# Evictions of the projections ahead of all other work on ScalarE and VectorE, in a fused three-layer graph attention kernel

## The chip, the cores and the metric

The kernel runs on one core of one Trainium2 chip, all in float32. The metric is the device time in microseconds (us). TensorE multiplies matrices into PSUM[...]; ScalarE and VectorE read results out of PSUM and do the element-wise work; GpSimd does element-wise work in SBUF; SyncE issues most DMAs.

## The reference

64 graphs of 256 nodes with 512 features each, and a 256x256 adjacency matrix per graph. Three attention layers follow each other; the second and the third belong to one reference layer.

```
Q, K, V = (x @ W + b) by 8 heads of 64
scores = Q K^T / 8 + a_i + c_j + b_g + log(adj + 1e-9)
x = softmax(scores) V + x

# twice: W1 with 8 heads, then W2 with one head of 512
h = layer_norm(x, g, b) @ W
s = h . a_src ; t = h . a_dst
e = leaky_relu(s_i + t_j, 0.2) + adj
x = softmax(e) h + x
```

## The kernel before

All 64 graphs go through one software pipeline on one core. `graph(b)` is a Python generator that traces the work of one graph and stops at each `yield`. A list, `order`, says which graph takes its next step; in the steady part it repeats the table `period`, whose entries are pairs (age, step): the steps of graphs of ages 0 to 5 are interleaved, so in each period every stage of some graph runs once. `start` and `finish` are lists of their own for the first and the last graphs.

TensorE executes exactly in the order in which its instructions are traced (`manual_schedule` for that engine). For ScalarE, VectorE, GpSimd and the DMA queue a planner makes the lists before the run: it walks a model of the program in time, and when an engine is free, it gives it, of the instructions whose inputs are there in that model, the one with the best priority. Without further marks priority is the order of tracing: what was traced earlier goes first. On the chip each engine then runs its fixed list in order and waits on semaphores.

Each projection (V, Q, K of the first layer, V1 of the second, V2 of the third) is one call of `winograd` (L310): a 2x2 block product done with seven products instead of eight, accumulated in three PSUM banks a, b and c. `product` (L322) issues the matmuls of one of the seven, on line L326 where the result lies by token (V, V1, V2) and L333 where it lies by column (Q, K). Between the products the banks are read out, and these readings are the evictions the change speaks of:

- `kept` (L339) copies a bank's intermediate sum into an SBUF tile (m1, m5, u2), since the bank goes on accumulating. Its instruction is on ScalarE: L525 for V and K, L558 for Q (two pieces), L639 for V1 and V2.
- `put` writes a finished block into V, QT, KT, V1 or V2. When a kept tile is to be added it is on VectorE (L537, L567, L575, L648); the last block of each projection, with nothing to add, goes over ScalarE (L535, L558, L573, L646).

The order in `winograd` is: products 1 into a, 5 into b, 2 into c, 6 into a, 3 into b (entry "K" in the table, for example), then 7 into a (entry "K7"), then 4 into a (entry "K4"). Product 6 adds to bank a and so must wait until m1 has been copied from it; product 7 likewise waits for u2, product 4 for the put of a.

Other work on the same two engines, by its lines:

- Scores of the first layer ("scores", "mask"): 16 matmuls for each half of the heads (L592), eight exponentials on ScalarE (L599), then on VectorE four multiplications by the adjacency (L613) and two sums over the halves, `total` (L618). `weight_sums` ("sums 0") sums `total` on TensorE into ps_su (L384); "product 0" multiplies by V into ps_num (L425); "gather 0" scales it on VectorE (L434, L438).
- Weights of the second layer ("weights", eight entries per period): for each head two ReLU of R on ScalarE (L676); after every second head VectorE adds the adjacency (L682) and ScalarE takes four exponentials (L686); after every fourth head VectorE sums the halves into R (L691), which ps_su reads in "sums 1". R comes by a DMA (L473) that the DMA queue issues when its buffer is free.
- Third layer: L744, the products with V2 into ps_av (L756), reciprocals (L761), scaling on ScalarE (L764), addition on GpSimd (L765).
- Statistics for the norms on VectorE (L258 to L290), among them "tokens" and "gather" entries; transposes of X and the adjacency (L501, "turn").

The order of the entries is the table's: in program order "Q4" and "K" come after the fourth "weights" and before the fifth, and "V2" comes between the two "mask" entries.

Of the kernel before, what the change touches and what calls it, by code (L numbers as in the profile page):

```python
# [20 lines left out]
def kernel(  # L21
# [130 lines left out]
    with ExitStack() as main:  # L152
# [6 lines left out]
        def ps(tag):  # L159

            return psum.tile([P, 512], F32, name=f"ps_{tag}", tag="ring", bufs=8)
# [148 lines left out]
        def winograd(left, w, by_token, keep, put, banks="cba"):  # L310

            width = HD if not by_token else w.shape[-1]
            bank = {n: ps(n)[:, :width] for n in banks}
            a, b, c = bank["a"], bank["b"], bank["c"]


            def product(n, to, first):  # L322
                A, B = left[n], w[:, :, FACTOR[n]]
                if by_token:
                    for kk in range(2):
                        nc.tensor.matmul(  # L326
                            to, A[:, kk, :], B[:, kk, :], start=(first and kk == 0),
                            stop=(kk == 1), skip_group_check=not first,
                        )
                else:  # L330
                    for m in range(2):
                        for kk in range(2):
                            nc.tensor.matmul(  # L333
                                to[:, m * P : (m + 1) * P], B[:, kk, m * P : (m + 1) * P],
                                A[:, kk, :], start=(first and m == kk == 0), stop=(kk == 1),
                                skip_group_check=True,
                            )

            def kept(name, src, row, column):  # L339
                k = work.tile([P, HD + H], F32, name=name, tag="kept", bufs=4)[:, :width]  # L340
                keep(k, src, row, column)
                return k

            product(1, a, True)
            m1 = kept("m1", a, 0, 0)
            product(5, b, True)
            m5 = kept("m5", b, 1, 1)
            product(2, c, True)
            put(c, m1, 0, 0)
            product(6, a, False)  # L350
            u2 = kept("u2", a, 0, 1)
            product(3, b, False)
            put(b, u2, 0, 1)
            yield
            product(7, a, False)
            put(a, m5, 1, 1)
            yield
            product(4, a, False)
            put(a, None, 1, 0)
            yield  # L360
# [116 lines left out]
        def graph(b):  # L477
# [62 lines left out]
            for _ in winograd(left, wv, True, copy, put_v, "abc"):  # L540
                yield
# [35 lines left out]
            for _ in winograd(  # L577
                left, wq, False, lambda d, s, r, c: keep_q(columns(d), columns(s), r, c), put_q
            ):
                yield  # L580
            for _ in winograd(left, wk, False, copy, put_k):
                yield
# [542 lines left out]
```

## Time and profile before

| what | value |
|---|---|
| time, median of 3 runs | 3233.33 us (3231.98 to 3235.2) |
| time of the profiled execution | 3234.22 us |
| its span, first to last instruction | 3232.4 us |
| granted TensorE clock, mean | 0.991 |
| TensorE matmul busy | 3135.6 us, 97% |
| VectorE busy | 2717.1 us, 84% |
| ScalarE busy | 2188.5 us, 68% |
| GpSimd busy | 1068.4 us, 33% |
| TensorE idle before ps_av, waiting for ET L744 | 24.3 us in 4 waits |
| HBM traffic | 125 GB/s over the span |

In the profile PE is TensorE's matmuls, PEld its weight loads, DVE VectorE, ACT ScalarE, POOL GpSimd. A group line gives the line of code, engine, operation, output<-inputs, shape and count; then busy time and mean ns of one; then the idle time of the engine just before these instructions and what ended it. A wait line gives who waited for whom, the total in us, how often, and the longest. A timeline line gives the start in us, the duration, and the instruction; in square brackets the idle time before it and what ended it. Busy time of matmuls overlaps between neighbours, since they are pipelined.

### The profile page before, as it was taken

Reading aid. Unit: us, or ns where it says so; the run is one execution under the profiler, and the core shown is the slowest. Engines: PE = TensorE matmul, PEld = TensorE weight load, DVE = VectorE, ACT = ScalarE, POOL = GpSimd, SP = SyncE. Lnnn points to the kernel's source line nnn. Section 1 sums busy time; section 2 is a strip of 40 time slices with the busy share of each in tenths; the row PEclk is TensorE's granted clock in tenths of the full one; section 3 lists DMA queues with packets and bytes.
Section 4 is the critical chain, followed back from the end, with each engine's and each line's share of the span. In section 5 each row is a group of like instructions: output and inputs, shape, how many; then the busy total and the mean of one; then the engine's idle time right before and its main releaser. Section 6 shows DMA issues by size and latency. Waiting matters only on the chain. (4 is left out here: it accounts for less than half of the span.)

```text
span 3232.4 us, 77827 instructions
## 1 busy us (share of the span) xinstructions
PE 3135.6 (97%) x28232; PEld 2621.6 (81%) x28232; DVE 2717.1 (84%) x6093; ACT 2188.5 (68%) x5959; POOL 1068.4 (33%) x1315
## 2 busy tenths in 40 slices
PE   7899999999999999999999999999999999999986
PEld 5678888888888888888888888888888888888864
DVE  5788888888888888888888888888888888888885
ACT  3467677677677677676676676676676676676673
POOL 3232332332332332333333333333323423423333
PEclk9999999999999999999999999999999999999998
DMA  4234444444444444444444444444444434444432
GB/s 133 92 118 131 124 131 131 126 127 133 127 128 133 127 124 135 128 122 134 129 122 136 125 126 124 131 130 125 132 124 132 132 123 133 131 123 133 125 116 90
DMA packets 354664, 407.94 MB, mean 126 GB/s; under 512 B 117840, under 2 KB 262496, under 8 KB 354272
## 3 DMA queue, kind: packets, MB, share of 16 engines
q1 hardware_dynamic: 353120, 401.83, 41.6%
q8 instruction: 224, 3.67, 0.5%
q14 instruction: 168, 1.38, 0.1%
q10 hardware_dynamic: 1152, 1.06, 0.1%
HBM read 266.83 MB, written 135.87 MB: 125 GB/s over the span
## 5 line engine op out<-in xcount | busy, mean ns | idle before, releaser
L682 DVE TENSOR_TENSOR ET<-ET,AT 128x512 f32<-128x512 f32 x512 | 363.4, 711 | 239.3 <-ACT ET L676 238.7
L686 ACT ACTIVATE ET<-ET,ends 128x256 f32<-128x256 f32 x1024 | 482.1, 503 | 104.7 <-DVE ET L682 103.6
L676 ACT ACTIVATE ET<-R,f 128x256 f32<-128x256 f32 x1024 | 461.3, 501 | 74.9 <-PE ps_num L425 55.7
L425 PE MATMUL ps_num<-ET,V 128*32 128x256 f32 x8192 | 466.7, 379 | 0.0
L302 POOL TENSOR_TENSOR S<-yT 128x256 f32<-128x256 f32 x64 | 47.7, 746 | 1210.5 <-ACT zT L409 967.6
L765 POOL TENSOR_TENSOR X<-X,weighted 128x256 f32<-128x256 f32 x256 | 210.9, 834 | 545.0 <-ACT weighted L764 536.9
L425 PEld LDWEIGHTS ps_num<-ET,V 128*32 128x32 f32 x8192 | 263.9, 110 | 155.2 <-issue 1.1
L613 DVE TENSOR_TENSOR ET<-ET,AT 128x1024 f32<-128x1024 f32 x256 | 306.6, 1231 | 39.4 <-ACT ET L599 39.4
L599 ACT ACTIVATE ET<-ps_sc,V 128x512 f32<-128x512 f32 x512 | 302.3, 697 | 7.8 <-PE ps_sc L592 7.8
L756 PE MATMUL ps_av<-V,ET 128*128 128x258 f32 (+1 forms) x1024 | 250.7, 389 | 24.3 <-DVE ET L744 24.3
L326 PE MATMUL ps_a<-w,S 128*128 128x264 f32 (+1 forms) x1024 | 268.5, 385 | 4.9 <-ACT m L639 2.9
L326 PE MATMUL ps_b<-w,S 128*128 128x264 f32 (+1 forms) x1024 | 266.6, 383 | 0.8 <-DVE w L131 0.7
L592 PE MATMUL ps_sc<-QT,KT 64*128 64x256 f32 x2048 | 239.4, 383 | 0.0
L263 DVE BATCH_NORM_STATS2 parts<-Z 128x6 f32<-128x128 f32 x1024 | 238.3, 275 | 0.1
L756 PEld LDWEIGHTS ps_av<-V,ET 128*128 128x128 f32 x1024 | 189.8, 196 | 48.9 <-issue 13.0
L326 PEld LDWEIGHTS ps_a<-w,S 128*128 128x128 f32 x1024 | 185.9, 189 | 46.7 <-ACT m L639 6.9
L326 PEld LDWEIGHTS ps_b<-w,S 128*128 128x128 f32 x1024 | 193.8, 189 | 32.5 <-PE ps_a L326 1.1
L592 PEld LDWEIGHTS ps_sc<-QT,KT 64*128 64x128 f32 x2048 | 192.4, 187 | 24.8 <-issue 1.5
L646 ACT ACTIVATE V<-ps_a,rstd 128x257 f32<-128x257 f32 (+1 forms) x128 | 60.0, 469 | 199.2 <-PE ps_a L326 199.2
L434 DVE TENSOR_TENSOR ps_num<-ps_num,R 128x512 f32<-128x512 f32 x256 | 169.9, 687 | 9.6 <-DMA R<-kept 7.0
L702 POOL TENSOR_TENSOR Z<-Z,bw 128x1024 f32<-128x1024 f32 x64 | 175.7, 2745 | 4.1 <-DVE parts L263 3.0
L409 ACT ACTIVATE yT<-yT,columns 128x256 f32<-128x256 f32 x256 | 120.8, 499 | 65.4 <-DMA yT<-kept 65.4
(175 smaller groups left out, 7396.3 us busy)
## 6 DMA issues: line engine op xcount, KB each, us to landing
R<-kept SPq DMA_DIRECT2D x128, 512.0 KB
X<-in_x_dram SPq DMA_DIRECT2D x256, 128.0 KB
kept<-xT SPq DMA_DIRECT2D x64, 512.0 KB
yT<-kept SPq DMA_DIRECT2D x64, 512.0 KB
R<-kept SPq DMA_DIRECT2D x512, 64.0 KB
kept<-yT SPq DMA_DIRECT2D x64, 512.0 KB
kept<-Z SPq DMA_DIRECT2D x64, 512.0 KB
X<-kept SPq DMA_DIRECT2D x512, 64.0 KB
```

Of the source, the lines that this page charges most:

```text
L263: nc.vector.bn_stats(parts[:, block].rearrange("p h c -> p (h c)"), Z[:, block, :])
L326: nc.tensor.matmul(to, A[:, kk, :], B[:, kk, :], start=(first and kk == 0), stop=(kk == 1), skip_group_check=not first,)
L425: nc.tensor.matmul(num[32 * a : 32 * a + 32, m * N : (m + 1) * N], V[:, j, a // 2, a % 2 * P + q * DH + 32 * m :][:, :32], pair[a // 2][:, ...
L592: nc.tensor.matmul(banks[h % 2][:, o : o + N], KT[lo : lo + DH, (q + h) // 2, j * P : (j + 1) * P], QT[lo : lo + DH, (q + h) // 2, :], sta ...
L599: nc.scalar.activation(ET[:, j, i::2, :], banks[i].rearrange("p (h n) -> p h n", n=N), AF.Exp, bias=c[:, j, :],)
L613: nc.vector.tensor_tensor(ET[:, j, :, :], ET[:, j, :, :], AT[:, j, :].unsqueeze(1).to_broadcast([P, 4, N]), ALU.mult,)
L676: nc.scalar.activation(ET[:, j, h, :], R[q][:, h, :], AF.Relu, bias=f[:, j, at : at + 1])
L682: nc.vector.tensor_tensor(two, two, AT[:, j, :].unsqueeze(1).to_broadcast([P, 2, N]), ALU.add)
L686: nc.scalar.activation(ET[:, j, i, :], ET[:, j, i, :], AF.Exp, bias=targets[:, j, 4 * q + i : 4 * q + i + 1],)
L702: nc.gpsimd.tensor_tensor(Z, Z, folded["2"].row.unsqueeze(1).to_broadcast([P, 2 * KC, P]), ALU.add)
L756: nc.tensor.matmul(av[:, :width], ET[:, j, t * P : (t + 1) * P], V2[:, j, n, :width], start=(j == 0), stop=(j == NT - 1),)
L765: nc.gpsimd.tensor_tensor(o[:, cols], o[:, cols], weighted, ALU.add)
```

## The change

Inside `winograd` the local names `put` and `kept` are wrapped: their instructions are now traced under `tc.high_priority()`, which gives them a priority ahead of everything traced outside such a block. It holds for all five projections of all graphs. The tiles are allocated as before, the instructions, their operands and engines are the same, and TensorE's list is the traced order as before.

```diff
@@ -336,9 +336,16 @@
                                 skip_group_check=True,
                             )
 
+            put_one = put
+
+            def put(*args):
+                with tc.high_priority():
+                    put_one(*args)
+
             def kept(name, src, row, column):
                 k = work.tile([P, HD + H], F32, name=name, tag="kept", bufs=4)[:, :width]
-                keep(k, src, row, column)
+                with tc.high_priority():
+                    keep(k, src, row, column)
                 return k
 
             product(1, a, True)
```

## The prediction

> **What bounds the kernel now.** I read the page first, then the TensorE groups, then the waits, then one period of the timeline engine by engine.
>
> ```profile
> span 3232.4 us, 77827 instructions
> ...
> PE 3135.6 (97%) x28232; PEld 2621.6 (81%) x28232; DVE 2717.1 (84%) x6093; ACT 2188.5 (68%) x5959; POOL 1068.4 (33%) x1315
> ...
> PE   7899999999999999999999999999999999999986
> ```
>
> TensorE is the bound: its busy time over the windows 300 to 1000, 1000 to 2000 and 2000 to 3000 us is 697.39, 991.30 and 995.40 us. About 48.9 us pass per graph. Evictions can only save what TensorE still waits, so I compare equal products:
>
> ```profile
> L333 PE MATMUL ps_a<-S,wk 128*128 128x128 f32 x1024 | 147.2, 287 | 17.2 <-ACT m L525 16.4
> ...
> L333 PE MATMUL ps_b<-S,wk 128*128 128x128 f32 x1024 | 135.6, 275 | 0.0
> ...
> PE ps_a L333 <- ACT m L525: 16.4, 27, 1.7
> ...
> ACT ET L676 <- DMA R<-kept: 18.9, 26, 3.4
> ```
>
> One product stands out: number 6 of K, written into bank a before ScalarE has copied m1 out of it. In the timeline the three products ahead of it start 0.89 us apart; the step from product 2 to product 6 is longer by 25.4 us summed over all 64 graphs, and the step to product 7, waiting for u2, by 3.6 us more. Of these 29.0 us some are counted as busy. Every other step repeats to within some ns. One graph with a long wait:
>
> ```profile
> 1779.67 1.06 PE L333 MATMUL ps_c<-xT,wk 128*128 128x128 f32 x8
> 1782.45 1.16 PE L333 MATMUL ps_a<-S,wk 128*128 128x128 f32 x8 [1.73 <-ACT m L525]
> ...
> 1779.14 1.71 ACT L676 ACTIVATE ET<-R,f 128x256 f32<-128x256 f32 x4 [1.54 <-DMA R<-kept]
> 1780.75 0.89 ACT L686 ACTIVATE ET<-ET,ends 128x256 f32<-128x256 f32 x2
> 1781.55 0.60 ACT L558 ACTIVATE QT<-ps_a,columns 128x128 f32<-128x128 f32 x2
> 1782.04 0.36 ACT L525 COPY m<-ps_a 128x256 f32<-128x256 f32 x1
> ```
>
> ScalarE's list puts four L676, two L686 and the two halves of the QT eviction ahead of m1. The first L676 waits for the DMA of R, and everything behind it, m1 included, is late by as much. QT's last matmul ended at about 1778.05 and m1's at 1778.94: both are ready long before they run.
>
> **What the Trainium skill says.** "PSUM — Partial Sum Buffer", section "Engine vs sequencer instructions": ScalarE and VectorE queues are strict FIFO, and matmuls start in program order. The trace agrees: m1 starts only after the L676 that waited 1.54 us, and TensorE waits behind product 6. "Perfetto Trace Analysis", section "Tensor Engine Instruction (MATMUL, LD_WEIGHTS)": matmul ends are estimated; so I count starts, which give 29.0 us where the named waits give less.
>
> **The change part by part.** No instruction, byte or buffer is added. Only the planner's choice among instructions that it holds ready at the same moment changes. So I ask where an eviction lost such a choice, and read it from program order (the table `period`) against executed order.
>
> Step 1, most of VectorE: nothing moves. An eviction that stands behind an instruction traced after it wasn't ready in the plan, and priority can't help. V's b (entry "V") stands behind L265 ("gather 1", later); V1's c behind L691 (the last "weights"); QT's b behind L434 ("gather 0"). V2's c is most telling: entry "V2" precedes the second "mask", yet that mask and its L618 run first. Cost 0.
>
> Step 2, K on ScalarE. The four L676 are "weights" entries traced after "Q4" and "K", and are ahead of QT in the list: QT wasn't ready in the plan then. They stay. The two L686 behind them belong to the "weights" entry before "Q4"; they won by priority, and now lose. The list becomes L676 four times, QT twice, then m1 with one or no L686 ahead: m1's product is one later on TensorE (0.89 us), QT's two pieces take 0.50 us (1781.55 to 1782.04), so a plan that fills the gap places one L686. An L686 costs 0.40 us (two from 1780.75 to 1781.55). m1 comes 0.40 us earlier with one L686 bypassed, 0.80 us with both. Taking from each of the 64 stalls at most 0.40 us gives 15.3 us, at most 0.80 us gives 21.8 us. I take 15.3 and keep both: the DMA and the four L676 stay in front.
>
> Step 3, what waits for the delayed L686. L691 follows them on VectorE and moves back about 0.9 us (QT 0.50 and m1 0.36). KT's c put (0.42 us) fills part. R is read by ps_su about 40 us later, and VectorE idles 0.45 us before rinv at 1542.10, ahead of the xT transposes; these end some 0.2 us before V's first product needs them. If that cover is gone, V's first product is late, by at most 0.9 − 0.45 − 0.2 = 0.25 us a graph, 16 us in all. I take 0.
>
> Step 4, scores. V4's put (L535, 0.25 us to the next start) and V2's m1 and m5 can pass the last of the eight L599. These end at 1514.5, and the last L613 starts at 1515.67: even 0.25 + 0.37 + 0.37 = 0.99 us fits in 1.17 us. Cost 0.
>
> Step 5, start and finish. In the first 300 us TensorE waits 4.4 us for QT L567, 1.7 for KT L575 and some 5 for single evictions; after 3000 us about 7. There the product chain of one graph is the path, but most waits are the eviction's own duration. I take 2 us of the 18; the bounds are −3 (orders written for the old lists) and 5.
>
> Sum: 15.3 + 2 = 17 us from the profiled execution's 3234.22 us (its span is 3232.4, 1.8 us lie around it). That execution stands 0.9 us over the median, 3233.33. So 3216 us on the median's scale.
>
> **The rivals.**
>
> Full removal: the plan also brings QT and m1 ahead of the L676. For it: m1, m5 and QT run back to back, so all were ready. Against: the L676 order of step 2. It gives 29.0 + 5: 3200 us.
>
> Nothing: in the plan QT only becomes ready after both L686, and the lists at K stay. For it: no executed order shows the plan's own instant. Against: m5, 1.8 us behind QT on TensorE, starts 0.75 us after QT without a later-traced filler between; QT must have waited. It gives 3233 us, give or take 6. Here the change doesn't do what it says.
>
> Slower: V2's c and b puts go ahead of the last `total` on VectorE, on which TensorE's list waits.
>
> ```profile
> 1515.67 1.22 DVE L613 TENSOR_TENSOR ET<-ET,AT 128x1024 f32<-128x1024 f32 x1
> 1516.92 1.23 DVE L618 TENSOR_TENSOR total<-ET 128x1024 f32<-128x1024 f32 x1
> 1518.07 0.48 DVE L648 SCALAR_TENSOR_TENSOR V<-ps_c,rstd,m 128x257 f32<-128x257 f32 x1
> ...
> 1517.31 1.03 PE L326 MATMUL ps_a<-w,S 128*128 128x257 f32 x4
> 1518.27 0.97 PE L384 MATMUL ps_su<-total,ones 128*32 128x128 f32 x28
> ```
>
> total ends at 1518.15 and ps_su starts at 1518.27; the update takes about 0.04 us, so the slack is 0.07 us. One put ahead (0.39 us to the next start) stalls TensorE by 0.32 us, two by 0.71 us; with 60 graphs and the 17 us won, that is 3236 us with one put and 3259 us with two. It decides from 17/60 = 0.28 us a graph. For it: on the chip c is ready at 1515.8, 1.1 us before total starts. Against: step 1, by which the plan held c unready until total was chosen. But the shifted lists upstream can turn this.
>
> **How the numbers follow.** About 0.2%, or 6.5 us, is what a measurement of this kernel can tell from no change. Forecast (0.48): 3216, own range 3208 to 3224. Full removal (0.14): 3200. Nothing (0.16): 3227 to 3239. Slower (0.22): mostly 3259, 0.03 of it the single put. Faster: nearly all of the first two, 0.62. Same: nothing plus the single put, 0.18. Slower: 0.20. The range runs from 3200, the full removal, to 3242, where the nothing case and the single put end; the two-put case, step 3's bound apart, is what is left out.
>
> **What would show it.** Right: the wait of ps_a L333 for m L525 under 6 us, m1 in ScalarE's timeline ahead of at least one of the two L686, the four L676 still in front, and ps_su still directly after total. Wrong: L648 between the last L613 and L618; a wait of ps_su for total of over 10 us; a wait of V's first product for xT; or the same list at K as now.

## The result, and the profile after

| | before | after |
|---|---|---|
| median of 20 runs each | 3235.03 us (3231.45 to 3241.38) | 3238.84 us (3233.02 to 3245.02) |
| ratio to before | | 1.0014, 95% interval 1.0008 to 1.002 |
| span of the profiled execution | 3232.4 us | 3238.2 us |

The forecast was 3216 us. The gain of 17 us didn't come; the kernel became slower by some 4 us, less than the 0.2% that the prediction names as what a measurement can tell, but the whole interval lies above 1. In the changed kernel every line behind the edit has a number higher by 7: m1, m5 and u2 of K are L532 now, QT's pieces L565, the ReLUs L683, the exponentials of the second layer L693, the eps on the adjacency L524.

The head of the page of the changed kernel (busy time and share of the span):

```profile
span 3238.2 us, 77766 instructions
...
PE 3135.7 (97%) x28232; PEld 2620.5 (81%) x28232; DVE 2722.7 (84%) x6093; ACT 2189.9 (68%) x5959; POOL 1051.8 (32%) x1315
```

TensorE's busy time is the same to 0.1 us, so the span grew by idle time. The groups of TensorE and the waits of all engines of the changed kernel say where K's idle time now is:

```profile
L333 PE MATMUL ps_a<-S,wk 128*128 128x128 f32 x1024 | 143.9, 284 | 19.8 <-ACT u L532 11.2 <-ACT m L532 6.0
...
L333 PE MATMUL ps_b<-S,wk 128*128 128x128 f32 x1024 | 135.3, 275 | 0.0
```

```profile
PE ps_a L333 <- ACT u L532: 11.2, 40, 0.5
...
PE ps_a L333 <- ACT m L532: 6.0, 10, 1.1
...
PE ps_su L391 <- DVE total L625: 3.0, 2, 2.0
```

The wait for m1 fell from 16.4 us in 27 to 6.0 in 10, close to the forecast of under 6. But u2, which had no line of its own, now has 40 waits, each of at most 0.5 us. The last line is for the slower rival: ps_su waits for `total` exactly as before.

To add it up I count starts of products, as the prediction did. Summed over the 64 graphs, from product 2 of K to the product after it (6), from there to product 7, and from there to the next step on TensorE:

| step | before | after |
|---|---|---|
| product 2 to 6, over 0.893 us each | 25.4 us | 9.9 us |
| product 6 to 7, over 1.786 us each | 13.1 us | 29.0 us |
| product 2 to the step after product 7, in all | 279.0 us | 280.0 us |

15.5 us are won ahead of product 6 and 15.9 are lost ahead of product 7, two products later. The 13.1 us of before are 3.6 from product 3 to 7, which is the stall that the prediction counted; 6.0 from product 6 to 3, a step that takes 0.995 us instead of 0.893 where product 6 has waited; and 3.5 of one graph in which a product with V2 lies between. After the change they are 22.8, 2.7 and 3.5, so the 29.0 of this table is not the prediction's 29.0. In this pair of profiles no step of TensorE's outside K differs by more than 0.2 us in sum over the stretch from 300 to 3000 us, and the two kernels need the same time for it to 0.2 us.

One graph each shows how. First ScalarE and TensorE in the timeline of before:

```profile
1534.77 1.71 ACT L676 ACTIVATE ET<-R,f 128x256 f32<-128x256 f32 x4 [0.51 <-DMA R<-kept]
1536.38 0.90 ACT L686 ACTIVATE ET<-ET,ends 128x256 f32<-128x256 f32 x2
1537.18 0.60 ACT L558 ACTIVATE QT<-ps_a,columns 128x128 f32<-128x128 f32 x2
1537.68 0.36 ACT L525 COPY m<-ps_a 128x256 f32<-128x256 f32 x1
1537.93 0.38 ACT L525 COPY m<-ps_b 128x256 f32<-128x256 f32 x1
1538.19 0.52 ACT L686 ACTIVATE ET<-ET,ends 128x256 f32<-128x256 f32 x1
1538.61 0.72 ACT L517 ACTIVATE AT<-AT,eps 128x512 f32<-128x512 f32 x1
1539.22 0.51 ACT L686 ACTIVATE ET<-ET,ends 128x256 f32<-128x256 f32 x1
1539.62 0.36 ACT L525 COPY u<-ps_a 128x256 f32<-128x256 f32 x1
...
1538.09 1.16 PE L333 MATMUL ps_a<-S,wk 128*128 128x128 f32 x8 [0.54 <-ACT m L525]
1539.08 1.06 PE L333 MATMUL ps_b<-S,wk 128*128 128x128 f32 x8
1540.03 1.16 PE L333 MATMUL ps_a<-S,wk 128*128 128x128 f32 x8
1541.03 1.90 PE L756 MATMUL ps_av<-V,ET 128*128 128x258 f32 x8
```

The same stage in the timeline of after:

```profile
1536.56 1.69 ACT L683 ACTIVATE ET<-R,f 128x256 f32<-128x256 f32 x4
1538.15 0.60 ACT L565 ACTIVATE QT<-ps_a,columns 128x128 f32<-128x128 f32 x2
1538.65 0.50 ACT L693 ACTIVATE ET<-ET,ends 128x256 f32<-128x256 f32 x1
1539.06 0.35 ACT L532 COPY m<-ps_a 128x256 f32<-128x256 f32 x1
1539.31 0.51 ACT L693 ACTIVATE ET<-ET,ends 128x256 f32<-128x256 f32 x1
1539.72 0.36 ACT L532 COPY m<-ps_b 128x256 f32<-128x256 f32 x1
1539.97 0.52 ACT L693 ACTIVATE ET<-ET,ends 128x256 f32<-128x256 f32 x1
1540.38 0.72 ACT L524 ACTIVATE AT<-AT,eps 128x512 f32<-128x512 f32 x1
1541.00 0.50 ACT L693 ACTIVATE ET<-ET,ends 128x256 f32<-128x256 f32 x1
1541.39 0.36 ACT L532 COPY u<-ps_a 128x256 f32<-128x256 f32 x1
...
1539.76 1.06 PE L333 MATMUL ps_a<-S,wk 128*128 128x128 f32 x8
1540.65 1.06 PE L333 MATMUL ps_b<-S,wk 128*128 128x128 f32 x8
1541.81 1.16 PE L333 MATMUL ps_a<-S,wk 128*128 128x128 f32 x8
1542.80 1.90 PE L763 MATMUL ps_av<-V,ET 128*128 128x258 f32 x8
```

The two lists hold the same instructions between the first ReLU and u2: four ReLUs, QT's pieces, m1, m5, four exponentials, the eps. Only their order differs. So m1 ends 2.85 us after the first ReLU begins instead of 3.27, but u2 ends 5.19 us after it, and 5.21 before. Product 7 begins 5.25 and 5.26 us after it. Over the steady graphs the median from the first ReLU to the end of u2 is 5.208 us before and 5.213 us after. ScalarE is busy without a gap all this time, and once product 6 waits less, TensorE only reaches u2's wait earlier.

### The profile page after: what moved, and what is told of

Same layout as the page of the kernel before. It is cut to its first block, busy times and chain, and to the rows that moved or that the text cites. A ratio compares the mean times of both kernels' runs of the same rounds, so it can differ in the third digit from the quotient of the medians.

```text
span 3238.2 us, 77766 instructions
## 1 busy us (share of the span) xinstructions
PE 3135.7 (97%) x28232; PEld 2620.5 (81%) x28232; DVE 2722.7 (84%) x6093; ACT 2189.9 (68%) x5959; POOL 1051.8 (32%) x1315
## 5 line engine op out<-in xcount | busy, mean ns | idle before, releaser
L693 ACT ACTIVATE ET<-ET,ends 128x256 f32<-128x256 f32 x1024 | 490.0, 505 | 107.1 <-DVE ET L689 106.0
L683 ACT ACTIVATE ET<-R,f 128x256 f32<-128x256 f32 x1024 | 461.7, 501 | 75.9 <-PE ps_num L432 55.6
L698 DVE TENSOR_TENSOR R<-ET 128x1024 f32<-128x1024 f32 x128 | 155.1, 1212 | 11.9 <-ACT ET L693 11.3
L771 ACT ACTIVATE weighted<-ps_av,rinv 128x256 f32<-128x256 f32 x256 | 114.5, 473 | 73.3 <-DVE rinv L768 57.5
```

The lines of the kernel that those rows point to most:

```text
L683: nc.scalar.activation(ET[:, j, h, :], R[q][:, h, :], AF.Relu, bias=f[:, j, at : at + 1])
L693: nc.scalar.activation(ET[:, j, i, :], ET[:, j, i, :], AF.Exp, bias=targets[:, j, 4 * q + i : 4 * q + i + 1],)
```

## The experiments

Ratios are to the kernel before on the same chip. "K's chain" is the sum from product 2 to the step after product 7 over the 64 graphs, as in the table above. It rests on one profile each; one kernel profiled twice gave 280.0 and 291.4 us (the change), another 255.7 and 249.0, so differences of some 10 us in it are not read. The position of a copy in ScalarE's list, counted from the first ReLU, scatters far less: to the end of u2 it is 5.213 us in the median in the first profile of the change and 5.208 in the second.

### Where in the run the loss sits: middle, ends

```diff
-                with tc.high_priority():
+                with tc.high_priority() if high else nullcontext():
...
+            return 7 <= b < B - 7
```

The last line is the condition for `high` in middle, so graphs 7 to 56 have the priority; in ends it is `not 7 <= b < B - 7`, the other 14. `put` and `kept` are treated alike.

> Priority only for graphs 7 to 56; the first and last seven as before. Theory 'given back': in the steady part the 15.5 us won at product 6 of K are lost again at product 7, since ScalarE's list up to u2 holds the same work; the 4 to 5 us of the whole change come from the first and last graphs. Then this one runs like the kernel before, ratio 0.9995 to 1.0005, with the wait of product 6 at about 10 us and that of product 7 above 20. Rival 'steady loss': the shifted lists cost some 0.07 us in every graph; then this one is as slow as the whole change, ratio 1.001 or more.

> Priority only for the first and the last seven graphs. 'Given back': all of the loss is here, ratio 1.001 to 1.002, and most of it after 3100 us of the span. 'Steady loss': like the kernel before, ratio within 0.0005 of 1.

Measured: middle 1.0002 (0.9993 to 1.0011), ends 1.0001 (0.9991 to 1.0012). The forecast gain is missing from the middle, which has 50 of the 64 graphs: there the m1 gain was forecast at about 12 us (50/64 of 15.3), and the interval leaves at most 2.3 (0.9993). In ends a loss of 0.1 to 0.2% was expected and did not show; neither half alone shows the small loss.

### u2 by itself: u2_first, all_u2_first

Where u2 is the limit, freeing it should bring the gain out. The first attempt moves much: the eps, all exponentials of the second four heads and the ReLUs of the last two heads stand behind u2 on ScalarE; all_u2_first is the same with the change. `behind_k(condition)` is a mark for the planner: what is traced under it comes on ScalarE behind the last K copy traced so far, u2. The eps is traced a little later for this.

```diff
-                nc.scalar.activation(AT, AT, AF.Identity, bias=eps)
...
+                with behind_k(True):
+                    nc.scalar.activation(AT, AT, AF.Identity, bias=eps)
...
+                        with behind_k(q == 1 and h >= 2):
...
+                                with behind_k(q == 1):
```

The last two edits are the ReLUs (L676) and the exponentials (L686).

> The kernel before, with the adjacency's +eps and the exponentials and later ReLUs of the second four heads put behind u2 of K on ScalarE; the four L676 and two L686 stay in front of m1. No eviction priority. 'Given back': m1 is where it was, so product 6 still waits some 25 us; u2 now follows m5, which only frees what product 7 waits, 7 to 13 us in all: 3220 to 3228 us, ratio 0.996 to 0.998. Rival 'the copies don't matter, VectorE does': the delayed exponentials hold up L682 and L691, and it is not faster than before, ratio 1.000 or more.

> The change, with the same work put behind u2 of K. 'Given back': now nothing takes back what m1 wins, so product 6 waits some 10 us and product 7 under 5: 25 to 35 us faster than the change, 3204 to 3214 us, ratio to before 0.990 to 0.994, and clearly faster than u2_first. Rival: if product 7's wait has another cause than the work ahead of u2 on ScalarE, it stays above 15 us and the ratio is 0.998 or more.

Measured: 1.0526 (1.0504 to 1.0547) and 1.0563 (1.0539 to 1.0587). In K the picture is the theory's: with u2 freed, the change takes K's chain from 270.0 to 253.2 us, where without that it took it from 279.0 to 280.0. The times are not. The timeline of u2_first shows the new wait, in V1, the next projection of another graph:

```profile
1577.35 0.35 ACT L535 COPY u<-ps_a 128x257 f32<-128x257 f32 x1
1579.40 0.91 ACT L705 ACTIVATE ET<-ET,ends 128x256 f32<-128x256 f32 x2 [1.70 <-DVE ET L700]
1580.21 0.46 ACT L656 ACTIVATE m<-ps_a,rstd 128x264 f32<-128x264 f32 x1
...
1577.75 1.05 PE L326 MATMUL ps_c<-w,yT 128*128 128x264 f32 x4
1580.73 1.16 PE L326 MATMUL ps_a<-w,S 128*128 128x264 f32 x4 [1.93 <-ACT m L656]
```

V1's m1 (L656 here) now stands behind two deferred exponentials (L705), and these wait for VectorE, which got the ReLUs' output later. The wait is 117.1 us in 62, of some 170 us that were lost. I had asked what the deferral frees and not what it starves. This pair settles K, and says nothing on the whole.

### Less deferred: eps2, all_eps2, k_eps2, k_only

Now only the eps and the last four ReLUs go behind u2; the exponentials stay free. Four kernels: that alone, with the change, with priority for K alone, and priority for K alone without it.

```diff
-                                with behind_k(q == 1):
...
+            return name == "K"
```

The first line is taken out of the edit of u2_first; the second is the condition for `high` in k_eps2 and k_only.

> The kernel before; only the adjacency's +eps and the ReLUs of the last two heads are put behind u2 of K on ScalarE, the exponentials stay where they were (the larger deferral of u2_first starved V1's m1). 'Given back': u2 comes 0.6 us earlier after m5, but m1 is where it was; product 6 still waits 25 us, K as a whole is 7 to 10 us shorter: ratio 0.997 to 0.998. Rival 'any deferral costs as much elsewhere': 1.000 or more, with a new wait at V1.

> The change with the same two things behind u2 of K. 'Given back': product 6 waits 10 us as in the change, product 7 under 8 instead of 29; K is 18 to 25 us shorter than in the change and the kernel 3214 to 3222 us, ratio to before 0.993 to 0.996. Rival 'any deferral costs as much elsewhere': 1.001, like the change.

> As all_eps2, but priority for the evictions of K alone. If what the change does in the steady part is all in K, as the lists say, this is as fast as all_eps2 within 0.1%, or faster by the 2 to 4 us that the lists of the first and last graphs cost. If the other four projections gain from priority, it is slower than all_eps2.

> The kernel before with priority for the evictions of K alone. 'Given back': product 6 waits about 10 us and product 7 about 29, K's sum is that of the kernel before within 2 us, ratio 0.9995 to 1.001. If a wait of another projection had made up for K's gain, this one keeps the 15 us: ratio 0.995.

| | K's chain | ratio (95%) |
|---|---|---|
| before | 279.0 us | 1 |
| the change | 280.0 us | 1.0014 (1.0008 to 1.002) |
| k_only | 284.0 us | 1.0001 (0.9992 to 1.0009) |
| eps2: u2 relieved alone | 275.9 us | 0.9981 (0.9974 to 0.9988) |
| all_eps2: both | 255.6 us | 0.9991 (0.9984 to 0.9997) |
| k_eps2: both, K alone | 255.7 us | 0.9961 (0.9947 to 0.9975) |

This is the clearest evidence for the cause. Moving m1 forward alone changes K's chain by +1.0 us (+5.0 for k_only), relieving u2 alone by −3.1 us, all within the scatter; both together change it by −23.4 us (−23.3 for k_eps2). ScalarE's median from the first ReLU to the end of u2 is 4.60 us in all_eps2 and k_eps2, where it was 5.21. In eps2, where 7 to 10 us had been expected in K, product 7 no longer stalls behind product 3, but product 6 still waits 30.5 us.

With priority for K alone, m1 comes forward by another way: both exponentials stay ahead of it, and QT's two pieces, which have no priority then, go behind it. So k_only is not the change's list, but a second way of moving m1 without moving u2: m1 ends 0.50 us earlier, u2 at 5.209 us, and nothing is gained.

Two forecasts failed here. all_eps2 was expected at 0.993 to 0.996: it has won 23 us in K and is hardly faster. And k_eps2 is 10.6 us faster than it in the medians, with the intervals apart, where at most 2 to 4 us were expected. In the steady part all_eps2 is 0.5 us ahead of before. What returned the gain are small steps behind K: the step to V's first product grew from 160 to 311 ns in the mean, V1's step after product 7 from 901 to 994 ns, four others by 0.03 to 0.04 us. Scaled to 64 graphs the first is 9.7 us and the second 5.9. In k_eps2 the first is smaller, 236 ns. The timeline of all_eps2, VectorE and TensorE:

```profile
1013.78 1.29 DVE L518 STREAM_TRANSPOSE xT<-X 128x512 f32<-128x512 f32 x2
...
1014.78 0.32 PE L268 MATMUL ps_st<-parts,same 128*128 128x48 f32 x2
1015.12 0.92 PE L329 MATMUL ps_a<-wv,xT 128*128 128x257 f32 x3
```

The transposes of X end at 1015.07 and V's first product starts 0.05 us later. TensorE has become early enough to find VectorE late.

### VectorE's stretch behind K: r_late, all_eps2_r_late, k_eps2_r_late

To test that, VectorE is relieved: the sum of the first four heads' weights (L691, 1.2 us) is taken out of the stretch ahead of the transposes and put behind V1's last put.

```diff
-                    if h == 3:
+                    if h == 3 and q == 1:
+                        with behind_put():
+                            nc.vector.tensor_tensor(R[0], pair[0][:, 0], pair[0][:, 1], ALU.add)
                         nc.vector.tensor_tensor(R[q], ET[:, 0], ET[:, 1], ALU.add)
```

> The kernel before with one sum on VectorE (R of the first four heads, 1.2 us, read some 40 us later) moved from ahead of the xT transposes to behind V1's last put. Theory 'VectorE is the next bound behind K': before the change TensorE waits for ScalarE's copies of K and not for VectorE, so taking 1.2 us out of VectorE's stretch ahead of xT changes little: ratio 0.998 to 1.001. Rival 'VectorE bounds the kernel before already': 0.995 or less.

> all_eps2 with the same sum moved. 'VectorE is the next bound': the 24 us that K gave up in all_eps2 and that came back at V's first product, at the products with V2 and at V1 are won for good: ratio to before 0.992 to 0.995, V's first product no longer waiting for xT. Rival 'the time comes back for another reason': it stays at 0.999.

> k_eps2 with the same sum moved: the fastest so far. 'VectorE is the next bound': 0.991 to 0.994, against 0.9961 without the move. Rival: no faster than k_eps2.

Measured: 1.0034 (1.0021 to 1.0046), 1.0044 (1.003 to 1.0058), 1.004 (1.0026 to 1.0054). The step to V's first product did come down, to 154 and 158 ns, but K's chain went up to 303.5 and 298.1 us. VectorE now delivered the inputs of two more exponentials early, and the planner put four instead of two between m5 and u2. The gap ahead of u2 had been filled again, here in k_eps2_r_late between m5 and u2:

```profile
1500.86 0.36 ACT L550 COPY m<-ps_b 128x256 f32<-128x256 f32 x1
1501.12 1.71 ACT L720 ACTIVATE ET<-ET,ends 128x256 f32<-128x256 f32 x4
1502.72 0.36 ACT L550 COPY u<-ps_a 128x256 f32<-128x256 f32 x1
```

As tests of VectorE all_eps2_r_late and k_eps2_r_late are void, and all three forecasts failed. r_late by itself kept its list at K, and K's chain (280.3 us); its profile lost 4.6 us in the first 275 us and 2 us from 300 to 3000. But that profile is of its fastest execution, 9.4 us under its median, so it doesn't show where most of the loss lies.

### The same with u2's list held: k_eps2_r2, all_eps2_r2, k_eps2_again

```diff
+                                with behind_k(q == 1 and h == 1 and j == 1):
                                     nc.scalar.activation(
                                         ET[:, j, i, :], ET[:, j, i, :], AF.Exp,
```

So ScalarE's list between the first ReLU and u2 is that of k_eps2 and of all_eps2 again, and VectorE's sum alone is moved. k_eps2 runs beside them on the same chip.

> Priority for K alone, the eps of the adjacency and the ReLU of the last two heads behind u2, the sum of the first four heads' weights moved on VectorE behind V1's last put, and the two exponentials that this frees kept behind u2 as well, so that ScalarE's list from R's landing to u2 is that of k_eps2. Theory (behind K the next bound is VectorE's stretch up to the xT transposes): the step to V's first product falls from 236 to about 155-160 ns a graph, K stays at 253-260 us from product 2 to the step after product 7 over 64 graphs, and the time is below k_eps2's by up to 5 us, ratio to before 0.993-0.996. Rival (the sum lands where its new place costs as much, or V1 steps take it back): V's first product comes down but the ratio is 0.996-1.000.

> The same with the priority of all projections (the change). Theory: the step to V's first product falls from 311 to about 155-160 ns, 9.7 us over 64 graphs come back, ratio to before 0.995-0.998 against 0.9991 in all_eps2. Rival: the remaining losses of all_eps2 (V1's step after product 7 901 to 994 ns, ps_av +5.2 us) belong to the priority and not to VectorE at K: ratio stays at 0.998-1.000.

> k_eps2 once more, on the same chip as the two others: ratio 0.9947 to 0.9975 as measured, V's first product 236 ns.

| | median | ratio (95%) | K's chain | V's first product, mean | over 200 ns |
|---|---|---|---|---|---|
| before | 3235.54 us | 1 | 279.0 us | 160 ns | 4 of 55 |
| k_eps2_again | 3226.26 us | 0.9969 (0.996 to 0.9979) | 249.0 us | 253 ns | 45 of 56 |
| k_eps2_r2 | 3218.04 us | 0.9943 (0.993 to 0.9957) | 249.6 us | 184 ns | 10 of 56 |
| all_eps2_r2 | 3214.58 us | 0.9935 (0.992 to 0.9949) | 250.2 us | 190 ns | 11 of 56 |

(The profile of before is the one shown at the start, not taken beside the other rows; all_eps2 had 55 of 55 over 200 ns.) The timeline of all_eps2_r2 at the same place:

```profile
1004.45 1.30 DVE L523 STREAM_TRANSPOSE xT<-X 128x512 f32<-128x512 f32 x2
...
1005.86 0.32 PE L268 MATMUL ps_st<-parts,same 128*128 128x48 f32 x2
1006.02 0.88 PE L329 MATMUL ps_a<-wv,xT 128*128 128x257 f32 x3
```

The transposes end 0.27 us ahead of the product instead of 0.05. With K's chain equal, k_eps2_r2 beats k_eps2_again with intervals apart, by 8.2 us in the medians, more than the 5 us I had expected. The two profiles lie further apart, since that of k_eps2_r2 is of its fastest execution (3210.16 us): of 14.6 us in their steady parts, scaled to 64 graphs, V's first product gives 4.4, V1's step after product 7 gives 3.8, the rest is spread over small steps. That step to 155 ns was expected and 184 measured, so the wait isn't gone in all graphs. The rival for all_eps2_r2, that its losses belong to the priority of the other projections, falls: with VectorE relieved it is as fast as k_eps2_r2. It has the lowest median of the study, 21 us below before. What the priority is worth inside it isn't measured: no kernel with u2 and VectorE relieved and without priority was run.

### The change once more: after_again

> The change itself once more, beside the others. 'Given back': its steady part is that of the kernel before; 1.000 to 1.002, product 6 at 10 us and product 7 above 20 us again.

Measured: 1.0019 (1.001 to 1.0027). The small loss is there in a second comparison too, with the order of K's list as in the first. But product 6 stalled for 17.6 us, not 10, and the steps from product 6 to 7 for 31.8. The profile, of the slowest of its 12 executions, has waits of 25.8 us in 32 for the DMA of R, where the first profile of the change has 19.5 in 25, and its steady part is 10.0 us longer than that of before as shown at the start, nearly all of it in K.

## Why the prediction was right or wrong

- **What bounds the kernel**: right in the place, K's product 6 behind ScalarE's list; incomplete in the question. The prediction saw u2's 3.6 us as a second, separate item of the 29.0 us. It is the same list's next deadline: u2's stall was small only because product 6 had already waited for the same list. The 29.0 us are also short of what K lost, since the steps behind a stalled product, which repeat just as well, are 0.10 us longer than the others.
- **Step 1, VectorE**: right in what it says of V2. ps_su's wait for `total` is 3.0 us in 2, as before; the slower rival did not occur.
- **Step 2, K on ScalarE**: here is the failed step. The list came out as forecast, one exponential bypassed, m1 earlier by 0.40 us in the mean over the steady graphs (its end from 3.05 to 2.65 us after K's product 1 begins), and the stalls ahead of product 6 fell by 15.5 us where 15.3 was forecast. What failed is to carry these 15.3 us into the sum as time of the kernel. The bypassed exponentials were still ahead of u2, so u2's end didn't move (5.00 us after product 1 in both), and product 7's stall rose by 15.9. The prediction asked what is late next of VectorE and not of the next copy in the same list. eps2 and all_eps2 show it from both sides: u2 relieved, the same edit is worth some 20 us of K's chain (275.9 to 255.6, one profile each), about twice the scatter.
- **Step 3, what waits for the delayed exponentials**: right in the place, the xT transposes ahead of V's first product, though the change alone doesn't reach it (160 ns before, 156 after). all_eps2 met it once K was faster: 0.15 us a graph at V's first product, under the bound of 0.25, and with V1 and the small steps 0.42 us a graph, nearly all that K had won. I took 0 in the sum. The cause is the delayed exponentials only in part, if at all: in k_eps2 both stay ahead of m1, and V's first product still comes later (236 ns). eps2 defers the same ReLUs as k_eps2 and hardly shortens K, and has 171 ns; so most of it comes with TensorE's being earlier.
- **Step 4, scores**: no step of TensorE's there changed; the cost 0 stands.
- **Step 5, start and finish**: wrong in sign, and small. In the profiles after is 2.3 us behind before at 300 us, and loses 3.4 us more after 3100 us. Of the latter 2.2 us are no wait: the last 16 matmuls with V2 take 6.09 us instead of 3.89, most of that time at half the granted clock (lines at the end of this document). This goes beyond the change: seven of the 17 profiles have it, with and without the priority, that of middle among them and that of ends not. Over the executions of after_again the mean clock is 0.989, and 0.991 in those of before beside them; in middle and ends it is that of before within 0.0002, and they lose nothing. Whether the change lowers the clock, or this is chance, isn't shown, and the cause of the 0.14% stays open. A share of the steady state isn't excluded either: this pair of profiles agrees to 0.2 us there, but middle's interval leaves up to 3.6 us (1.0011) for 50 graphs.
- **The rivals**: "nothing" gave the right time (3227 to 3239) by a wrong mechanism, since the lists at K did change. "Full removal" did not occur. In the chances the single put's 0.03 makes "same" 0.19 and "slower" 0.19, where 0.18 and 0.20 are written; nothing depends on it. A rival "the wait moves from m1 to u2" was missing. The Trainium skill's strict FIFO queues ("PSUM — Partial Sum Buffer", section "Engine vs sequencer instructions"), which the prediction cites, are where it could have been found: if a list is worked off in order, a new order among the same entries decides who is served first, and leaves the sum ahead of the last one as it is, here 5.2 us.

## What to carry to other kernels

When a stalled engine waits twice behind the same in-order list, price the last wait. Where that one is late as well, as here, moving the first forward gained nothing while the work ahead of the last was unchanged, so look for work that can go behind it. Whoever defers work must follow it to its consumer, and whoever frees a gap must see what the planner puts into it: both cost more here than they had brought. A gain that vanishes may still be there: the same change, with the next two limits removed, was part of a kernel 0.65% (0.51 to 0.8%) faster, though its own share in that was not measured.

## What the hardware showed beside it

A product of K that has waited costs more than its wait. In the timeline of before, product 6 waits and the next one starts 0.99 us after it, in that of after it doesn't and the next starts 0.89 us after it. From 300 to 3000 us this step is 995 ns in all 56 graphs of before, whether product 6 had waited 0.06 us or over 0.8 us; in after it is 995 ns in the 20 graphs with a wait of over 0.02 us and 909 ns in the mean in the other 36. So 0.10 us a wait is lost on top, however short the wait, which the named idle time doesn't contain. V's first product shows less: where it is late by 0.15 us in the mean (all_eps2), the step behind it is longer by 0.03 us (941 to 973 ns).

The granted clock falls only near the ends. In both profiles it is 1.00 from 300 to 3000 us, 0.96 in the first 300 us, and 0.93 (before) and 0.91 (after) from 3000 us on. The stretches at half clock last 3.4 to 13.7 us, and one of them decides what the last 16 matmuls of the products with V2 take, first in before, then in after:

```profile
3219.07 3.89 PE L756 MATMUL ps_av<-V,ET 128*128 128x258 f32 x16 [0.66 <-DVE ET L744]
...
3222.20 6.09 PE L763 MATMUL ps_av<-V,ET 128*128 128x258 f32 x16 [0.66 <-DVE ET L751]
```

Over the first group the mean clock is 1.00, over the second 0.61. All 17 profiles of this study have one of the two: 3.9 us at full clock in ten, 6.1 to 6.5 us in seven. So before a difference of some 2 us between two profiles is put down to a kernel, the clock in this place is to be compared.
